# An image pipeline with medians and an attention: the pace of the inverse transform, the counts of the median, the engine of its masks

## The chip, the core and the metric

The kernel runs on one core of one Trainium2 chip. Its engines are TensorE (PE; weight loads are listed as PEld), VectorE (DVE), ScalarE (ACT), GpSimd (POOL) and SyncE (SP, which here only issues transfers). Each takes its instructions in a fixed order; what passes between them goes through semaphores. The metric is the device time of one launch in microseconds (us), with the median of several runs. The profile is of one execution more.

## What is computed

The input x is 16 images of 64 channels, 128 by 128, in float32. Layer 0 shifts each channel by its median where that is negative, doubles the resolution with a 7-tap filter, rectifies, and filters and halves it again. Layer 1 filters in the frequency domain and then runs an attention over all 16,384 pixels of an image with 320 keys.

```python
# layer 0
q_in = jnp.quantile(x.reshape(B, C, -1), 0.5, axis=-1)
x = x + jax.nn.relu(-q_in)[:, :, None, None]
y = upfirdn2d(x, lpf, up=2, padding=lpf.shape[0] - 1, gain=4.0)
y = jnp.maximum(y, 0.0)
x = upfirdn2d(y, lpf, down=2, padding=0, gain=1.0)
# layer 1
spec = jnp.fft.rfft2(x, norm='ortho')
mag = jnp.abs(spec)
hid = jax.nn.gelu(jnp.einsum('bchw,oc->bohw', mag, fg_w1), approximate=False)
gate = jax.nn.sigmoid(jnp.einsum('bchw,oc->bohw', hid, fg_w2))
xf = x + jnp.fft.irfft2(spec * gate, s=(h, w), norm='ortho')
...
out = (attention of the queries from xf over keys and values from strided convolutions of xf)
return out @ proj_w + proj_b + x
```

## The kernel before

There are two phases. `phase1` makes z (layer 0's output, stored in `zd`) and xf (stored in `xfd`); `phase2` is the attention. The change touches `phase1` alone.

**Units.** A group is four channels of one image (G = 4, so NG = 16 groups per image). Partitions hold image rows or, later, frequencies. The program's main loop runs over steps u; an image has U = 32 of them, two per group, and v = u % 32 is the step within the image.

**A group's way.** `load` (L351) brings the group's four channels into one of four "pad" buffers by a GpSimd transfer (L355), and GpSimd adds the shift (L357). `up_cols` (L362) filters along the columns into `up`: two ScalarE instructions (L372), five on VectorE (L374). `up_rows`, once per half group, multiplies by the filter matrix on PE (L384, L393) and rectifies on ScalarE into `r` (L386) and `rc` (L395). `down_rows` goes back with PE (L407, L410) and copies y on ScalarE (L413), once per half group. `down_cols` (L415) makes z in seven VectorE instructions (L424, L426) and stores it through SP's queue (L429). `fourier_rows` (L437, copied at L439) and `fourier_cols` (PE at L448 to L451, copied by ScalarE into `sp`, L453) make the spectrum; 22 of these `sp` buffers exist. In a step the program writes down `load` for the group two ahead and `up_cols` for the group one ahead.

**The gate.** `gate(b)` is a generator, begun in step v = 5 of the next image, one piece per step. For each group it squares and adds (L463 on ScalarE, L465 and L466 on GpSimd) and takes the root into `mag` (L467, ScalarE). Then come PE transposes and two small products, and a sigmoid into `gt` (L515, L523). `mag` and `gt` of all images share one buffer (tag "maggt").

**The inverse.** For a group, `open_gate` (L530) works on GpSimd: 1 + gate (L534), the product with both parts of the spectrum (L536, two instructions), two small ones (L538, L539). It is kept behind the newest shift (`issue_after`). `inverse_cols` is 8 products on PE (L549) and a copy `bt` (L557); `inverse_rows` 4 more (L568), a ScalarE copy into `xf` (L576, two buffers) and the store by GpSimd's queue (L579). In the loop a group goes through these three in successive steps, one group per step: the gates of groups 0 to 15 are opened in steps 14 to 29 of the image after.

**The medians.** `medians(b)` is a generator for two images (128 channels on 128 partitions). SP loads both halves of the pixels into `xm` (L169; one buffer each, 2 MB per transfer, four transfers). A first guess comes from 2,048 pixels. Then `count` (L183: four VectorE passes of 4,096 values, each with its sum) counts the values under a threshold: twice for the two ends, then FINE = 5 times, with a new threshold from a secant each time (L270 to L275, L280 to L282). The last threshold t lies within a few ranks of the median. For each of 16 slices of 1,024 values (NS = 8 per half) VectorE then masks what is not below t (L289, L290) and takes the eight largest (L292); all this uses one buffer (tag "hit"), which the counts use too. From these candidates come the two middle values (L297 to L306). A flag says if some row ended more than 7 ranks off or hid a candidate; it goes through memory (L317, L319, L321), is read by VectorE's sequencer, and where it is set a full bitwise `search` of 33 counts follows. Last the shift is written and spread over the partitions (L334, L336, `sb`). `medians(0)` runs alone before the loop; the others are written down piece by piece in the steps from every even image on, for the images two ahead.

**The order.** The program text gives priorities; the order of the instructions on each engine is laid out when the kernel is built, by a planner that goes by those priorities and by when it thinks that operands and buffers are ready. So a piece can stand well before its place in the text: in the trace a median's L272 stands between two passes of the count written before it, and the last median is done when about 9 of the 16 images are.

Of the kernel before, what the change touches and what calls it, by code (L numbers as in the profile page):

```python
# [8 lines left out]
F32 = mybir.dt.float32  # L9
# [3 lines left out]
ALU = mybir.AluOpType  # L13
# [4 lines left out]
B, C, H, W = 16, 64, 128, 128  # L18
# [12 lines left out]
PAD = 3  # L31
# [2 lines left out]


GOAL, MISS = RANK + 9, 7
FINE = 5
BIG = 3.0e38


# [89 lines left out]
def phase1(ctx, tc, nc, cs, ident, x, w1, dram, zd, xfd):  # L130

    G = 4
    NG = C // G
    wp = ctx.enter_context(tc.tile_pool(name="p1w", bufs=1))
    big = ctx.enter_context(tc.tile_pool(name="p1big", bufs=1))
# [3 lines left out]
    io = ctx.enter_context(tc.tile_pool(name="p1io", bufs=3))  # L139
# [21 lines left out]
    def medians(b):  # L161
# [3 lines left out]
        for f in range(2):  # L165
            t = big.tile([128, HALF], F32, name=f"xm{b}_{f}", tag=f"xm{f}")
# [33 lines left out]
            nc.vector.tensor_scalar(less, total, float(RANK), None, ALU.is_gt)  # L200
            return less

        NS = 8
        L = HALF // NS

        def search(low, high):
# [49 lines left out]
        for f in range(2):  # L256
            hit = big.tile([128, FEW], F32, name=f"more{b}_{f}", tag="hit")
# [26 lines left out]
        cand = small.tile([128, 16 * NS], F32, name=f"cand{b}", tag="cand")  # L284
        for f in range(2):
            for s in range(NS):
                up = big.tile([128, L], F32, name=f"down{b}_{f}{s}", tag="hit")
                cut = xm[f][:, s * L : (s + 1) * L]
                nc.vector.tensor_scalar(up, cut, t, -BIG, ALU.is_ge, ALU.mult)  # L289
                nc.vector.tensor_tensor(up, up, cut, ALU.add)  # L290
                j = 8 * (NS * f + s)
                nc.vector.max(cand[:, j : j + 8], up)  # L292
                if s % 2:
                    yield
        top = small.tile([128, 16], F32, name=f"top{b}", tag="top")
        rest = big.tile([128, 16 * NS], F32, name=f"rest{b}", tag="hit")
# [46 lines left out]

    shifted = []
    pads = []
    for i in range(4):
        t = wp.tile([128, G, W + 2 * PAD], F32, name=f"pad{i}", tag=f"pad{i}")
        nc.gpsimd.memset(t, 0.0)
        pads.append(t)

    def load(b, g):  # L351

        c0 = G * g
        xi = pads[g % 4][:, :, PAD : PAD + W]
        nc.gpsimd.dma_start(out=xi, in_=x[b, c0 : c0 + G].rearrange("c h w -> h c w"))  # L355
        shifted.append(
            nc.gpsimd.tensor_tensor(  # L357
                xi, xi, shifts[b][:, c0 : c0 + G].unsqueeze(2).to_broadcast([128, G, W]), ALU.add
            ).ins
        )  # L360

    def up_cols(b, g):  # L362

        src = pads[g % 4]
        up = work.tile([128, G, UP], F32, name=f"up{b}_{g}", tag="up")
        for odd in range(2):
            o = up.rearrange("p g (m t) -> p g m t", t=2)[:, :, :, odd]
            for j in range(4 - odd):
                s = src[:, :, PAD - j : PAD - j + UP // 2]
                w = taps[:, 2 * j + odd : 2 * j + odd + 1]  # L370
                if j == 0:
                    nc.scalar.activation(o, s, AF.Copy, scale=w)  # L372
                else:
                    nc.vector.scalar_tensor_tensor(o, s, w, o, ALU.mult, ALU.add)  # L374
        us[b, g] = up
# [39 lines left out]
    def down_cols(b, g):  # L415
        n = f"{b}_{g}"
        c0 = G * g
        y = ys.pop((b, g)).rearrange("p g (m t) -> p g m t", t=2)
        z = io.tile([128, G, W], F32, name=f"z{n}", tag="z")
        for k in range(7):  # L420
            s = y[:, :, k // 2 : k // 2 + W, k % 2]
            w = taps[:, 6 - k : 7 - k]
            if k == 0:
                nc.vector.tensor_scalar(z, s, w, None, ALU.mult)  # L424
            else:
                nc.vector.scalar_tensor_tensor(z, s, w, z, ALU.mult, ALU.add)  # L426
        zv = zd[b][c0 : c0 + G].rearrange("c h w -> h c w")
        for at, h, m in HOME:
            nc.sync.dma_start(out=zv[h : h + m], in_=z[at : at + m])  # L429
        zs[b, g] = z  # L430
# [129 lines left out]
    def inverse_rows(b, g):  # L560
        n = f"{b}_{g}"
        c0 = G * g
        bt = bts.pop((b, g))
        o_ps = banks(f"ops{n}")
        for r in range(2):
            for i in range(2):
                half = slice(64 * i, 64 * i + 64)
                nc.tensor.matmul(  # L568
                    o_ps[:, i, 0:256],
                    cs("ihs" if r else "ihc")[half],  # L570
                    bt[half, r].rearrange("p q w -> p (q w)"),
                    start=(r == 0),
                    stop=(r == 1),
                )
        xf = io.tile([128, G, W], F32, name=f"xf{n}", tag="xf", bufs=2)
        nc.scalar.copy(  # L576
            xf.rearrange("p (q i) w -> p i q w", i=2), o_ps[:, :, 0:256].rearrange("p i (q w) -> p i q w", q=2)
        )
        nc.gpsimd.dma_start(out=xfd[b][c0 : c0 + G].rearrange("c h w -> h c w"), in_=xf)  # L579
# [12 lines left out]
        load(0, g)  # L592
    up_cols(0, 0)
    running, net = None, None
    for u in range(B * U + FIRST + NG + 2):
        b, v = u // U, u % U
        if v == 0 and b % 2 == 0 and b + 2 < B:
            running = medians(b + 2)
# [9 lines left out]
        w = u - FIRST - U  # L608
        for k, stage in ((-1, open_gate), (0, inverse_cols), (1, inverse_rows)):
            q = w - k  # L610
            if q >= 0 and q % U < NG and q // U < B:

                with tc.issue_after(shifted[-1]) if k < 0 else nullcontext():
                    stage(q // U, q % U)
        if v % 2 == 0 and at(u + 2):
            up_cols(*at(u + 2)[:2])
        if at(u):
# [444 lines left out]
```

## Time and profile before

| what | us |
|---|---|
| median of three runs (11609.7 to 11617.6) | 11612.71 |
| the profiled execution, its own time | 11611.63 |
| its span | 11609.8 |
| VectorE busy, whole span | 8352.8 |
| PE busy, whole span | 10189.2 |
| GpSimd busy, whole span | 2502.4 |
| first y copied (ScalarE, L413) | 307.9 |
| last median's flag read (L321) | 3457.6 |
| last y copied | 5284.4 |

The profile is one execution, taken by the hardware profiler. Engine names are as above. A row gives line, engine, operation, output and input with partitions x elements, and a count; then busy time and the mean of one in ns, then the idle time of the engine just before these instructions and who ended it. The row of one tile has minimum, median and maximum of one in ns instead. Rows of waits have the total in us, how often, and the longest. A stage's row gives, for each engine, the busy us and the number of instructions, then the clock that was granted to PE as a share of the full one, and the share and rate of the DMA engines. A wait is put down to what came last by the records, which is now and then not the true cause.

### The profile page before, as it was taken

The numbers are of one execution on the slowest core, as the hardware profiler recorded it, in microseconds if no ns is written. First come the engines' busy times: TensorE is split into PE (matmuls) and PEld (weight loads), VectorE is DVE, ScalarE is ACT, GpSimd is POOL, SyncE is SP. The second block draws the span as 40 slices with busy tenths as digits, with TensorE's granted clock in tenths as the row PEclk, the third lists the DMA queues.
The fourth block names the chain that finished last, engine by engine and source line by source line (L and its number), as shares of the span: only waits on it lengthen the run. The fifth ranks groups of instructions, "written<-read, shape, count | busy, mean of one in ns | idle before, by whom it ended". The sixth has DMA issues, their size and how long they took to land.

```text
span 11609.8 us, 175376 instructions
## 1 busy us (share of the span) xinstructions
PE 10189.2 (88%) x68096; PEld 4603.2 (40%) x68096; DVE 8352.8 (72%) x12025; ACT 5524.1 (48%) x7585; POOL 2502.4 (22%) x3370
## 2 busy tenths in 40 slices
PE   0668777787889999996999999999999999999999
PEld 0445444444445555553333333333333333333333
DVE  6978879779795555551777767767777677676777
ACT  0435444444445555552444545545445455454555
POOL 0224333343334444442000000000000000000000
PEclk9889888888889999998999999999999999999999
DMA  2121221221211111113212121121121211210111
GB/s 54 38 61 48 57 67 40 66 62 41 64 40 48 48 47 48 45 45 86 61 34 61 38 58 38 39 58 37 33 63 39 58 37 38 58 39 30 37 39 31
DMA packets 462689, 560.44 MB, mean 48 GB/s; under 512 B 80904, under 2 KB 344464, under 8 KB 459536
## 3 DMA queue, kind: packets, MB, share of 16 engines
q1 hardware_dynamic: 396304, 347.68, 13.2%
q0 software_dynamic: 65536, 201.39, 5.6%
q8 instruction: 538, 8.81, 0.3%
q14 instruction: 311, 2.55, 0.1%
HBM read 343.36 MB, written 201.33 MB: 47 GB/s over the span
## 4 chain that ended last, share of the span: by engine, by line
PE 48%; ACT 5%; DMA 1%; DVE 1%; SPq 1%; issue 1%; POOL 1%; ACTq 0%; POOLq 0%; DVEq 0%
PE av L791 13%; PE ma L791 13%; PE ss L791 12%; ACT e L881 4%; PE qp L791 3%; PE pj L791 2%; PE cp L704 2%; SPq L682 1%; PE bps L549 0%; DMA q<-nt 0%; DMA xp<-xfd 0%; DVE sd L728 0%; POOL sp L536 0%; PE rps L384 0%; PE yps L407 0%
## 5 line engine op out<-in xcount | busy, mean ns | idle before, releaser
L791 DVE TENSOR_REDUCE nm<-ma 128x2 f32<-128x640 f32 x4096 | 3240.9, 812 | 1272.1 <-PE ss L791 804.2
L881 ACT ACTIVATE e<-ss 128x1024 f32<-128x1024 f32 x2560 | 2620.7, 1024 | 2840.1 <-PE ss L791 2812.7
L791 PE MATMUL ss<-q,kg 32*128 32x512 f32 (+1 forms) x12288 | 2843.4, 635 | 32.5 <-DMA q<-nt 32.3
L791 PE MATMUL ma<-kg,q 32*128 32x320 f32 x16384 | 2763.6, 475 | 21.3 <-DVE nm L791 19.5
L791 PEld LDWEIGHTS ma<-kg,q 32*128 32x128 f32 x16384 | 1187.4, 185 | 1543.8 <-ACT e L881 803.9
L791 PE MATMUL av<-e,vb 128*32 128x512 f32 (+1 forms) x10240 | 1673.5, 610 | 0.0
L384 PE MATMUL rps<-up,w1s 128*128 128x262 f32 x4096 | 1116.3, 412 | 632.5 <-DVE up L374 367.6
L426 DVE SCALAR_TENSOR_TENSOR z<-y,w1s,z 128x512 f32<-128x512 f32 x1536 | 1314.1, 856 | 31.6 <-DVEq L324 3.1
L374 DVE SCALAR_TENSOR_TENSOR up<-pad,w1s,up 128x524 f32<-128x524 f32 x1280 | 976.9, 809 | 410.1 <-ACT up L372 330.7
L791 PEld LDWEIGHTS ss<-q,kg 32*128 32x128 f32 (+1 forms) x12288 | 728.4, 166 | 1293.6 <-DVE nt L791 397.6
L384 PEld LDWEIGHTS rps<-up,w1s 128*128 128x128 f32 x4096 | 767.7, 199 | 890.2 <-DVE up L374 307.2
L407 PE MATMUL yps<-r,w1s 128*64 128x262 f32 x4096 | 629.5, 422 | 364.1 <-ACT xf L576 337.9
L932 POOL DMA_DIRECT2D result<-ot x512 | 267.4, 527 | 2785.6 <-DVE ot L791 2751.7
L807 POOL COPY xo<-xa 128x512 f32<-128x512 f32 x256 | 272.1, 1064 | 2529.3 <-issue 2319.8
L386 ACT ACTIVATE r<-rps 128x524 f32<-128x524 f32 x1024 | 609.9, 611 | 337.4 <-PE rps L384 337.1
L183 DVE TENSOR_SCALAR_CACHE_REDUCE hit<-xm,t 128x4096 uint8<-128x4096 f32 x160 | 715.8, 4474 | 2.5
L357 POOL TENSOR_TENSOR pad<-pad,sb 128x512 f32<-128x512 f32 x256 | 302.7, 1183 | 1362.6 <-DMA pad<-x 1064.1
L549 PE MATMUL bps<-csb,sp 128*64 128x256 f32 x4096 | 565.1, 424 | 33.0 <-POOL sp L538 33.0
L424 DVE TENSOR_SCALAR z<-y,w1s 128x512 f32<-128x512 f32 x256 | 138.6, 541 | 584.9 <-ACT y L413 580.9
L407 PEld LDWEIGHTS yps<-r,w1s 128*64 128x64 f32 x4096 | 268.4, 144 | 726.7 <-ACT xf L576 377.6
L467 ACT ACTIVATE mag<-q 128x260 f32<-128x260 f32 x256 | 167.8, 655 | 790.9 <-POOL q L466 527.0
L355 POOL DMA_DIRECT2D pad<-x x256 | 200.6, 784 | 1584.6 <-DVE up L374 444.9
(151 smaller groups left out, 11481.5 us busy)
## 6 DMA issues: line engine op xcount, KB each, us to landing
xm<-x SPq DMA_DIRECT2D x32, 2048.0 KB
pad<-x POOLq DMA_DIRECT2D x256, 256.0 KB, 5.3
xfd<-xf POOLq DMA_DIRECT2D x256, 256.0 KB, 5.1
xp<-xfd SPq DMA_DIRECT2D x128, 512.0 KB
xa<-xfd SPq DMA_DIRECT2D x512, 128.0 KB
zr<-zd SPq DMA_DIRECT2D x512, 128.0 KB
result<-ot POOLq DMA_DIRECT2D x512, 128.0 KB, 2.9
zd<-z SPq DMA_DIRECT2D x512, 122.0 KB
```

The lines of the kernel that those rows point to most:

```text
L183: nc.vector.tensor_scalar(hit, cut, thr, None, op, ALU.add, accum_out=cnt[:, j : j + 1])
L357: nc.gpsimd.tensor_tensor(xi, xi, shifts[b][:, c0 : c0 + G].unsqueeze(2).to_broadcast([128, G, W]), ALU.add).ins
L374: nc.vector.scalar_tensor_tensor(o, s, w, o, ALU.mult, ALU.add)
L384: nc.tensor.matmul(r_ps[:, i, 0:UP], ut[:, STAGES[k]], up[:, 2 * p + i, :], start=True, stop=True)
L386: nc.scalar.activation(t, r_ps[:, :, 0:UP], AF.Relu, scale=4.0)
L407: nc.tensor.matmul(y_ps[half, i, 0:UP], dr, r[k][:, i, :], start=True, stop=True)
L426: nc.vector.scalar_tensor_tensor(z, s, w, z, ALU.mult, ALU.add)
L549: nc.tensor.matmul(b_ps[64 * i : 64 * i + 64, 256 * q : 256 * q + 256], s[:, r, 2 * q + i, 0:64], cs("iv2" if r else "iv1"), start=(r == 0 ...
L791: last[engine] = op(*args, **kw).ins
L807: nc.gpsimd.tensor_copy(xo.rearrange("p (a e f) -> p a f e", e=8, f=16), xas[b, p].rearrange("p (a f e) -> p a f e", e=8, f=16),)
L881: nc.scalar.activation(e, s_ps, AF.Exp)
L932: nc.gpsimd.dma_start(out=ov[h][:, cut], in_=ot[64 * h : 64 * h + 64, :])
```

## The change

In the loop the inverse runs at two groups in every three steps: group 2k in step 3k and group 2k + 1 in step 3k + 1, so that 16 groups take 24 steps and the gates are opened in steps 14 to 36. The main loop gets eight steps more at its end for that. The medians count six times instead of seven (FINE = 4). The slices are half as long and twice as many (NS = 16, 32 slices of 512 values), their mask's two instructions go from VectorE to GpSimd and get a buffer of their own (tag "down", one), and a piece is now four slices instead of two, still eight pieces. There are three pads in place of four, taken in turn over the images' borders; z has two buffers in place of three, xf three in place of two.

```diff
--- before.py
+++ after.py
@@ -34,7 +34,7 @@
 
 
 GOAL, MISS = RANK + 9, 7
-FINE = 5
+FINE = 4
 BIG = 3.0e38
 
 
@@ -200,7 +200,7 @@
             nc.vector.tensor_scalar(less, total, float(RANK), None, ALU.is_gt)
             return less
 
-        NS = 8
+        NS = 16
         L = HALF // NS
 
         def search(low, high):
@@ -284,13 +284,13 @@
         cand = small.tile([128, 16 * NS], F32, name=f"cand{b}", tag="cand")
         for f in range(2):
             for s in range(NS):
-                up = big.tile([128, L], F32, name=f"down{b}_{f}{s}", tag="hit")
+                up = big.tile([128, L], F32, name=f"down{b}_{f}{s}", tag="down")
                 cut = xm[f][:, s * L : (s + 1) * L]
-                nc.vector.tensor_scalar(up, cut, t, -BIG, ALU.is_ge, ALU.mult)
-                nc.vector.tensor_tensor(up, up, cut, ALU.add)
+                nc.gpsimd.tensor_scalar(up, cut, t, -BIG, ALU.is_ge, ALU.mult)
+                nc.gpsimd.tensor_tensor(up, up, cut, ALU.add)
                 j = 8 * (NS * f + s)
                 nc.vector.max(cand[:, j : j + 8], up)
-                if s % 2:
+                if s % 4 == 3:
                     yield
         top = small.tile([128, 16], F32, name=f"top{b}", tag="top")
         rest = big.tile([128, 16 * NS], F32, name=f"rest{b}", tag="hit")
@@ -343,7 +343,7 @@
 
     shifted = []
     pads = []
-    for i in range(4):
+    for i in range(3):
         t = wp.tile([128, G, W + 2 * PAD], F32, name=f"pad{i}", tag=f"pad{i}")
         nc.gpsimd.memset(t, 0.0)
         pads.append(t)
@@ -351,7 +351,7 @@
     def load(b, g):
 
         c0 = G * g
-        xi = pads[g % 4][:, :, PAD : PAD + W]
+        xi = pads[(NG * b + g) % 3][:, :, PAD : PAD + W]
         nc.gpsimd.dma_start(out=xi, in_=x[b, c0 : c0 + G].rearrange("c h w -> h c w"))
         shifted.append(
             nc.gpsimd.tensor_tensor(
@@ -361,7 +361,7 @@
 
     def up_cols(b, g):
 
-        src = pads[g % 4]
+        src = pads[(NG * b + g) % 3]
         up = work.tile([128, G, UP], F32, name=f"up{b}_{g}", tag="up")
         for odd in range(2):
             o = up.rearrange("p g (m t) -> p g m t", t=2)[:, :, :, odd]
@@ -416,7 +416,7 @@
         n = f"{b}_{g}"
         c0 = G * g
         y = ys.pop((b, g)).rearrange("p g (m t) -> p g m t", t=2)
-        z = io.tile([128, G, W], F32, name=f"z{n}", tag="z")
+        z = io.tile([128, G, W], F32, name=f"z{n}", tag="z", bufs=2)
         for k in range(7):
             s = y[:, :, k // 2 : k // 2 + W, k % 2]
             w = taps[:, 6 - k : 7 - k]
@@ -572,7 +572,7 @@
                     start=(r == 0),
                     stop=(r == 1),
                 )
-        xf = io.tile([128, G, W], F32, name=f"xf{n}", tag="xf", bufs=2)
+        xf = io.tile([128, G, W], F32, name=f"xf{n}", tag="xf")
         nc.scalar.copy(
             xf.rearrange("p (q i) w -> p i q w", i=2), o_ps[:, :, 0:256].rearrange("p i (q w) -> p i q w", q=2)
         )
@@ -592,7 +592,7 @@
         load(0, g)
     up_cols(0, 0)
     running, net = None, None
-    for u in range(B * U + FIRST + NG + 2):
+    for u in range(B * U + FIRST + 3 * NG // 2 + 2):
         b, v = u // U, u % U
         if v == 0 and b % 2 == 0 and b + 2 < B:
             running = medians(b + 2)
@@ -608,10 +608,10 @@
         w = u - FIRST - U
         for k, stage in ((-1, open_gate), (0, inverse_cols), (1, inverse_rows)):
             q = w - k
-            if q >= 0 and q % U < NG and q // U < B:
+            if q >= 0 and q % U < 3 * NG // 2 and q % U % 3 < 2 and q // U < B:
 
                 with tc.issue_after(shifted[-1]) if k < 0 else nullcontext():
-                    stage(q // U, q % U)
+                    stage(q // U, 2 * (q % U // 3) + q % U % 3)
         if v % 2 == 0 and at(u + 2):
             up_cols(*at(u + 2)[:2])
         if at(u):
```

## The prediction

> **What bounds the kernel now.** I read the page first (its 40 slices), then the busy time by stage, then in each stage the waits by engine, then single rows. One table gives the stages:
>
> ```profile
> core 0: us, PE busy (x) PEld busy (x) DVE busy (x) ACT busy (x) POOL busy (x), PEclk, DMA share, GB/s
> 0.00:290.00 290.00, 0.00 (x0) 0.00 (x0) 195.02 (x197) 1.28 (x1) 5.32 (x12) 1.00 0.26 54
> 290.00:3450.00 3160.00, 2431.61 (x13725) 1474.89 (x13725) 2649.86 (x3178) 1440.96 (x2533) 1068.98 (x1373) 0.87 0.22 54
> 3450.00:5290.00 1840.00, 1689.18 (x10160) 1022.78 (x10158) 1012.30 (x1272) 1040.75 (x1827) 824.47 (x1084) 0.96 0.16 46
> 5290.00:5500.00 210.00, 106.69 (x661) 57.41 (x663) 15.40 (x30) 45.54 (x66) 60.73 (x110) 0.73 0.44 103
> 5500.00:11609.00 6109.00, 5961.74 (x43558) 2048.15 (x43552) 4480.25 (x7350) 2995.52 (x3160) 542.89 (x792) 0.98 0.18 44
> ```
>
> The reader is to see five stages. Up to 290 the first median runs alone. From 290 to 3450 the seven other medians run beside the images: 300 copies of y by ScalarE fall there, so a half group takes 3160/300 = 10.53 us. From 3450 to 5290 no median is left: 212 half groups, 8.68 us each, PE busy 1689 of 1840 (92%). Then the inverse of the last image, and the attention, which the change leaves alone. At the later pace 300 half groups would take 2604 us, so the medians cost at most 556 us of the second stage; that is the prize. Inside it, four stretches of counting (770 us in all) show VectorE busy 761 and PE 568, and five stretches of masks (530 us) VectorE 509, PE 438, GpSimd 227. VectorE is the bound while it counts; under the masks PE is near its own limit too. Between two medians nearly everything stands, for transfers and behind them:
>
> ```profile
> DVE sums L253 <- DMA xm<-x: 187.1, 11, 25.7
> ...
> ACT xf L576 <- DMA xfd<-xf: 105.0, 19, 14.5
> ...
> PE yps L407 <- ACT xf L576: 278.8, 48, 29.2
> ...
> ACT mag L467 <- POOL q L466: 365.7, 99, 19.6
> ```
>
> These are waits of the second stage (total us, times, longest). ScalarE has waited 105 us for a buffer of xf to be stored, and PE 279 us for y's partner behind such a copy.
>
> **The change, part by part.** All sums stand against the profiled execution: 11611.63 us with a span of 11609.8; the median of the runs, 11612.71, is 1.1 above it. The prices of the median are in these rows (the first three of the second stage, the others over phase 1):
>
> ```profile
> L290 DVE TENSOR_TENSOR down<-down,xm 128x1024 f32<-128x1024 f32 x112 | 144.1, 1287 | 0.7
> L292 DVE MAX8 cand<-down 128x8 f32<-128x1024 f32 x112 | 136.4, 1218 | 0.7
> ...
> L289 DVE TENSOR_SCALAR down<-xm,t 128x1024 f32<-128x1024 f32 x112 | 92.8, 828 | 0.7
> ```
>
> ```profile
> L357 POOL TENSOR_TENSOR pad<-pad,sb x256: 1028/1035/3173, 290.9 to 5174.0; 128x512 f32<-128x512 f32 x128
> ```
>
> ```profile
> L534 POOL TENSOR_SCALAR gt<-gt 128x260 f32<-128x260 f32 x256 | 255.4, 1005 | 29.0 <-ACT gt L523 29.0
> L465 POOL TENSOR_TENSOR q<-sp 128x260 f32<-128x260 f32 x256 | 195.7, 769 | 138.8 <-ACT sp L453 136.9
> ```
>
> (1) The first median. One count is four passes of 4.48 us plus the small steps to the next threshold; in the timeline the rounds begin at 95.04 and 115.53, so one count less gives 20.5 us. Masks and maxima ran from 195.14 to 248.11, 53.0 us for 16 slices of 1,024. Now there are 32 slices of 512, and with one buffer named "down" each goes strictly round: mask on GpSimd (two instructions), maximum on VectorE, then the next mask. The tensor-tensor at 512 is between 1.03 us (L357, quietest) and 1.42 (L536's 0.72 at 260 elements, scaled). No GpSimd row has a tensor-scalar with two operations and a pointer. Quiet L534 takes 0.85 us at 260; to 512 elements that is 1.26 by the slope of the two-input rows (1.03 less 0.62, the quiet L465, for 252 elements) or 1.67 in proportion; if the second operation doubles it, 3.3. The maximum at 512 is 0.68, on the line between 1.22 at 1,024 and 0.28 at 128. Two hand-overs make 0.1 (a GpSimd result reached ScalarE in 0.04). A slice is thus 3.1 to 3.9 us, 5.5 if doubled; 32 of them 98 to 124 us, 177 if doubled. Net: +25 to +50, at worst +104. I take +37: single-operation rows are the nearest. Nothing covers this: no image can begin before its shift.
>
> The GpSimd rule speaks against the move. The Trainium skill ("GPSIMD Engine Reference", 4.1 Engine selection) sends elementwise work to VectorE, with GpSimd about twice as slow for two inputs; its section 3.1 gives 4497 ns for 2,048 elements, so 1.12 us for 512 by proportion, an estimate. By that price alone the 32 additions of a median would cost 3 us more than by L357's row.
>
> (2) Counts in the second stage: seven medians, 20 us of VectorE each, from stretches where VectorE is 99% busy and PE 74%. A stretch of about 192 us becomes 172 with PE at 83%, still under the 92% of the later stage, so the time comes back whole: −140. Bounds: 0 if transfers set the medians' pace anyway, −140.
>
> (3) Masks in the second stage: VectorE loses (144.1+136.4+92.8)/7 = 53.3 us per median and keeps 32 × 0.68 = 21.8. But in those stretches (106 us each) PE is busy 87.6; at 92% it needs 95. At most 11 us per median come back: −77. Bounds 0 and, were VectorE alone the bound, 7 × 31.5 = −220.
>
> (4) What the masks bring to GpSimd: 32 × (2.3 to 3.1) = 73 to 99 us per median, beside the 45 us that it already does in such a stretch. Over the stage GpSimd goes from 1069 of 3160 to about 1700: not a bound by total. But GpSimd and VectorE now pass one buffer to and fro 32 times, both in fixed order. Behind a waiting maximum stand z and up on VectorE, for which PE waits; behind a waiting mask stand the pad load's issue and shift, the gate's opening and xf's store. The nearest row for an engine that waits for a GpSimd pair is ScalarE's mag: 365.7 us for the 150 of this stage, 2.4 us each. ScalarE is 46% busy and often has nothing else; VectorE is full, and its order has z and up to put in between. I take a quarter, 0.6 us for each of 224 maxima: +134. Bounds 0 and 2.4 × 224 = +546.
>
> The two engines also slow each other. L536 has a median of 720 ns and a maximum of 1719, L374 739 at least and 1553 at most, and the timeline has such pairs side by side near 1090. The same page (8. Key points) names it: a shared SBUF interface, contended by VectorE instructions with two SBUF inputs. No sum here uses the rule; the rows are in the +134.
>
> (5) A third buffer for xf: ScalarE's waits for its store, 105.0 us, and 47.7 in the later stage, would mostly go. Behind them PE lost up to 278.8 and 59.1, though some of that has other causes and part comes back as the next wait, for pad or xm. I take −65 (about 35 of the later stage's 59, 30 before). Bounds 0 and −153.
>
> (6) The pacing. No instruction is added or removed. The later stage has 151 us of idle PE, 92 without the waits of (5), much of it in steps that had no inverse in them; the 16 inverse groups now fill 24 of 32 steps. Against it: the gate array and the magnitudes share one buffer, and its last reader moves from step 29 to 36, one step ahead of the next gate. More than the present 8 of the 16 magnitudes then come in a burst (1.08 us of ScalarE, about 1.4 of GpSimd each) in which PE loses about 8 us. I take −20; bounds −92 and +100 (6 us for each of 16 images).
>
> (7) Three pads and two z. In the later stage a pad load starts as soon as its pad's last reader ends (3851.05, then 3851.62), so up to three groups ahead, and takes some 7 us with its shift; at two groups ahead 17 us of a slack of about 45 are lost. With two buffers z is written again 29 us after it was finished (3845.4, 3874.1); its Fourier rows are done by 3866.3, and its store, whose landing no row shows, is half the size of xf's, which lands in 5.1. The cover is gone where xm jams the DMA (one pad load took 47.5 us): +5, bounds 0 and +50.
>
> Sum: 37 − 140 − 77 + 134 − 65 − 20 + 5 = −126. 11611.6 − 126 = **11,485 us**.
>
> **The rivals.**
> *VectorE stands at the maxima* (the slow side). If each of the 224 maxima waits 1.8 us (three quarters of mag's row), (4) is 403 and not 134: 11,485 + 269 = **11,755**. It decides from 260/224 = 1.16 us per maximum on (260 being all gains less all other losses). For it: the 1159–1185 stretch, where ScalarE waited 24.55 us for an opened gate that was itself queued on GpSimd behind a pad's 17.81 us wait; more GpSimd work lengthens such queues. Against: fillers.
> *VectorE was the bound throughout*: then all 7 × 51.5 = 361 us come back, xf's 153 too, with half of (4): 11,611.6 + 37 − 361 − 153 + 67 − 20 + 5 = **11,187**. For it: VectorE at 96% even under the masks. Against: PE at 83% there.
> *Hidden anyway*: transfers (187 us for xm, 105 for the flags' way through memory) set how fast medians follow; (2), (3) and (5) give nothing, (4) nothing either. Left are 37 − 20 + 5: **11,634**.
> *It does not do what it says*: with six counts a row could end over 7 ranks off, and the full search would run, 33 counts of 20 us, some 650 us. I followed the counts in float32 on the reference's input: the furthest of the 1,024 rows ends 6 off, so no search. 1 in 100.
>
> **How the numbers follow.** Forecast 0.50, standing maxima 0.27, VectorE throughout 0.13, hidden 0.09, search 0.01. The time is the forecast's, 11,485. The range leaves out about 1 in 10 on each side: 11,210 (just past the fast rival's time) to 11,780 (just past the slow one). The forecast's own range, its mid values varied singly, is 11,350 to 11,620. 0.2% is 23 us, about what can be told from no change. Faster: 0.44 of the forecast's 0.50 and all 0.13, so 0.57; no change: 0.03 of the forecast, 0.04 of hidden and 0.01 of the standing maxima, 0.08; slower: the rest, 0.35.
>
> **What would show it.** Right: the first pad shift starts at 320 to 345 instead of 290.9; L183 has 192 passes instead of 224; the mask rows on POOL have means of 2.3 to 3.1 us together; the last median's flag comes well before 3457; waits for xfd in front of xf fall under 50 us; VectorE's waits in front of its maximum stay under 200 us. Wrong: over 260 us there; a mask pair over 4 us; mag's waits for sp over the present 263; a later stage slower than 8.68 us per half group, which would put the fault with the pacing and the shared buffer; or any search.

## The result, and the profile after

The changed kernel takes 11939.66 us (median of four runs, 11936.31 to 11947.19) against 11614.1 for the kernel before beside it: ratio 1.0281, 95% interval [1.0264, 1.0299], 326 us slower. The forecast was 11,485, with a range up to 11,780: direction and range were both missed. The profiled span is 11934.5. The stages of the trace, in the columns used before (the second ends with the last median's flag, which fell at 3600.3 instead of 3457.6; it is cut 17 us before the first shift, which adds 0.06 us to each y below):

```profile
core 0: us, PE busy (x) PEld busy (x) DVE busy (x) ACT busy (x) POOL busy (x), PEclk, DMA share, GB/s
0.00:318.00 318.00, 0.00 (x0) 0.00 (x0) 146.40 (x160) 1.28 (x1) 108.31 (x74) 1.00 0.18 38
318.00:3600.00 3282.00, 2260.48 (x12212) 1382.67 (x12212) 2217.01 (x2722) 1302.80 (x2260) 1679.85 (x1654) 0.82 0.20 48
3600.00:5612.00 2012.00, 1910.95 (x11583) 1163.86 (x11583) 1220.59 (x1469) 1200.78 (x2091) 1003.69 (x1247) 0.97 0.16 49
```

The second stage makes 269 copies of y in 3282 us, 12.20 each where it was 10.53. VectorE, which was to be relieved and so let PE go faster, is busy 68% of it instead of 84%, PE 69% instead of 77%, GpSimd 51% instead of 34%. Over the whole stage nobody is the bound by busy time; everybody waits. The later stage has become better: 243 copies in 2012 us, 8.28 each where it was 8.68. So the loss is in the stage with medians, but for some 45 us in front of the first shift. The stretches in which the masks are used show more than the stage. These are sums over the seven later medians, each from its first maximum to its last, before and then after:

```profile
sum 769.04, PE 644.91 PEld 391.08 DVE 729.32 ACT 396.93 POOL 304.92; mean PE 92.13 PEld 55.87 DVE 104.19 ACT 56.70 POOL 43.56
```

```profile
sum 1237.34, PE 775.78 PEld 474.16 DVE 632.00 ACT 433.99 POOL 1071.97; mean PE 110.83 PEld 67.74 DVE 90.29 ACT 62.00 POOL 153.14
```

84 copies of y fall into the first and 89 into the second: 468 us more for about the same work on the images. VectorE was the full engine there (95%, GpSimd 40%); now GpSimd is (87%, VectorE 51%). The stage's waits, VectorE's, then PE's, then ScalarE's (total us, times, longest):

```profile
DVE cand L292 <- POOL down L290: 601.3, 195, 14.5
DVE sums L253 <- DMA xm<-x: 194.7, 11, 27.7
DVE z L424 <- DMA zd<-z: 74.3, 11, 13.3
```

```profile
PE fps L437 <- DVE z L426: 553.1, 70, 30.5
...
PE yps L407 <- ACT xf L576: 79.0, 18, 11.5
```

```profile
ACT y L413 <- DVE z L426: 463.5, 63, 30.3
...
ACT mag L467 <- POOL sp L536: 185.6, 7, 37.4
```

The two rows behind z were, in the stage before:

```profile
PE fps L437 <- DVE z L426: 142.9, 28, 12.6
```

```profile
ACT y L413 <- DVE z L426: 117.4, 24, 13.0
```

VectorE stands 601 us in front of its maxima, 2.7 us for each of the 224 of this stage. PE's wait for z has grown from 142.9 to 553.1, ScalarE's from 117.4 to 463.5: z stands behind the maximum on VectorE. Two things went as wanted: PE's wait behind xf fell from 278.8 to 79.0, and in this stage no wait of xf for its store is left. The tile of the masks (ns: minimum, median, maximum), and who held it up:

```profile
L289 POOL TENSOR_SCALAR down<-xm,t x256: 1991/2346/3104, 155.8 to 3578.1; 128x512 f32<-128x512 f32 x128
L290 POOL TENSOR_TENSOR down<-down,xm x256: 1252/1265/1721, 157.9 to 3581.2; 128x512 f32<-128x512 f32 x128
L292 DVE MAX8 cand<-down x256: 671/695/697, 160.1 to 3583.4; 128x8 f32<-128x512 f32 x128
its engine sat idle before it (us, times) until:
  POOL down L290: 697.5, 223
  DVE t L275: 151.9, 3
  DVE cand L292: 140.7, 142
```

Two stretches of the timeline show the round trip (start, us, engine and line, and in brackets the idle time before it with its releaser). In the first median, with nothing else on the chip:

```profile
204.25 0.69 DVE L292 MAX8 cand<-down 128x8 f32<-128x512 f32 x1 [3.47 <-POOL down L290]
205.04 2.00 POOL L289 TENSOR_SCALAR down<-xm,t 128x512 f32<-128x512 f32 x1 [0.83 <-DVE cand L292]
207.12 1.26 POOL L290 TENSOR_TENSOR down<-down,xm 128x512 f32<-128x512 f32 x1
208.41 0.69 DVE L292 MAX8 cand<-down 128x8 f32<-128x512 f32 x1 [3.47 <-POOL down L290]
```

and beside the images, VectorE alone:

```profile
3509.12 1.06 DVE L426 SCALAR_TENSOR_TENSOR z<-y,w1s,z 128x512 f32<-128x512 f32 x1
3512.34 0.69 DVE L292 MAX8 cand<-down 128x8 f32<-128x512 f32 x1 [2.16 <-POOL down L290]
3512.95 1.83 DVE L426 SCALAR_TENSOR_TENSOR z<-y,w1s,z 128x512 f32<-128x512 f32 x2
3516.93 0.69 DVE L292 MAX8 cand<-down 128x8 f32<-128x512 f32 x1 [2.15 <-POOL down L290]
3517.54 0.73 DVE L426 SCALAR_TENSOR_TENSOR z<-y,w1s,z 128x512 f32<-128x512 f32 x1
3521.52 0.69 DVE L292 MAX8 cand<-down 128x8 f32<-128x512 f32 x1 [3.25 <-POOL down L290]
```

A quiet slice takes 4.17 us (204.25 to 208.41): 2.00 + 1.26 on GpSimd, 0.69 on VectorE, and small gaps. Later VectorE has fillers (z), but only one or two between two maxima, and z's seven instructions are spread over several slices. One z began at 3532.60 and had five of its seven instructions behind it at 3544.38; by the medians of its instructions (486 ns for L424, 752 for L426) its seven take 5.0 us. PE's L437 waits for its end.

### The profile page after: what moved, and what is told of

The parts are those of the page before. It is cut to its first block, busy times and chain, and to the rows that moved or that the text cites. A ratio compares the mean times of both kernels' runs of the same rounds, so it can differ in the third digit from the quotient of the medians.

```text
span 11934.5 us, 176032 instructions
## 1 busy us (share of the span) xinstructions
PE 10252.5 (86%) x68096; PEld 4660.6 (39%) x68096; DVE 8080.5 (68%) x11729; ACT 5551.7 (47%) x7585; POOL 3398.2 (28%) x3881
## 4 chain that ended last, share of the span: by engine, by line
PE 59%; ACT 6%; POOL 3%; DVE 2%; issue 2%; DMA 1%; SPq 1%; ACTq 0%; DVEq 0%; POOLq 0%
PE av L791 13%; PE ma L791 13%; PE ss L791 12%; ACT e L881 4%; PE rps L384 3%; PE qp L791 3%; PE pj L791 2%; PE cp L704 2%; PE yps L407 2%; PE bps L549 2%; PE yps L410 1%; PE fps L437 1%; PE ops L568 1%; PE cps L393 1%; DMA pad<-x 1%
## 5 line engine op out<-in xcount | busy, mean ns | idle before, releaser
L384 PE MATMUL rps<-up,w1s 128*128 128x262 f32 x4096 | 1134.6, 419 | 527.4 <-DVE up L374 466.0
L426 DVE SCALAR_TENSOR_TENSOR z<-y,w1s,z 128x512 f32<-128x512 f32 x1536 | 1377.2, 897 | 43.8 <-DVEq L324 8.0
L374 DVE SCALAR_TENSOR_TENSOR up<-pad,w1s,up 128x524 f32<-128x524 f32 x1280 | 997.8, 833 | 248.1 <-ACT up L372 244.2
L384 PEld LDWEIGHTS rps<-up,w1s 128*128 128x128 f32 x4096 | 779.9, 202 | 823.6 <-DVE up L374 389.4
L437 PE MATMUL fps<-csb,z 128*128 128x128 f32 x2048 | 375.4, 339 | 586.9 <-DVE z L426 553.1
L289 POOL TENSOR_SCALAR down<-xm,t 128x512 f32<-128x512 f32 x256 | 593.8, 2320 | 300.7 <-DVE t L275 151.9
L413 ACT COPY y<-yps 128x524 f32<-128x524 f32 x512 | 305.6, 597 | 753.2 <-DVE z L426 463.5
L292 DVE MAX8 cand<-down 128x8 f32<-128x512 f32 x256 | 177.5, 693 | 697.5 <-POOL down L290 697.5
L424 DVE TENSOR_SCALAR z<-y,w1s 128x512 f32<-128x512 f32 x256 | 136.3, 532 | 694.5 <-ACT y L413 596.0
L437 PEld LDWEIGHTS fps<-csb,z 128*128 128x128 f32 x2048 | 318.1, 237 | 685.3 <-DVE z L426 430.8
```

What stands on the lines that cost most here:

```text
L289: nc.gpsimd.tensor_scalar(up, cut, t, -BIG, ALU.is_ge, ALU.mult)
L384: nc.tensor.matmul(r_ps[:, i, 0:UP], ut[:, STAGES[k]], up[:, 2 * p + i, :], start=True, stop=True)
L413: nc.scalar.copy(ys[b, g][:, 2 * p : 2 * p + 2, :], y_ps[:, :, 0:UP])
L437: nc.tensor.matmul(f_ps[:, 128 * i : 128 * i + 128], z[:, i, :], cs("fh"), start=True, stop=True)
```

## The experiments

Times are given against the kernel before in the same series of runs (11,601 to 11,616), with the ratio's 95% interval. They fall into four questions.

### Which part of the change loses the time?

`masks_on_vector` is the kernel after with L289 and L290 on VectorE again, all else as in the change:

```diff
-                nc.gpsimd.tensor_scalar(up, cut, t, -BIG, ALU.is_ge, ALU.mult)
-                nc.gpsimd.tensor_tensor(up, up, cut, ALU.add)
+                nc.vector.tensor_scalar(up, cut, t, -BIG, ALU.is_ge, ALU.mult)
+                nc.vector.tensor_tensor(up, up, cut, ALU.add)
```

> The changed kernel with the two mask instructions back on VectorE, all else kept (six counts, pacing, 32 slices, buffers). Theory HANDOVER: the loss is made where VectorE stands at each maximum for GpSimd's mask, 697.5 us over the eight medians; without that wait the kernel falls below the kernel before: its own gain in the stage after the medians, 0.4 us for each of 512 half groups (205), plus about 20 us for each of eight counts less (160), so 11,614 - 365 = 11,250, range 11,180 to 11,350. Rival PACING-OR-BUFFERS: the stage with medians is slow because of the later inverse, three pads or two z buffers (VectorE waited 74 us for the store of z there); then it stays above 11,614, near 11,800.

Measured: 11417.26, 0.9839 [0.9823, 0.9856], 191 us faster than before and 516 better than the change against it. The masks' engine is the whole loss and more. HANDOVER's range (11,180 to 11,350) was still missed: the rest of the change gains less than it took.

The other parts were put into the kernel before one by one. `masks_alone` has NS = 16, the masks on GpSimd in their own buffer, and three pads; `pacing_alone` only the two groups in three steps; `six_counts_alone` only FINE = 4; `xf_buffers_alone` two buffers for z and three for xf; `three_parts` is all but the masks (counts, pacing, z and xf; four pads and NS = 8 kept).

> The kernel before with only the mask's move to GpSimd, 32 slices and their own buffer (and three pads, which make the room for it): seven counts, no pacing, three z, two xf. Theory BOTH: the first median grows by 65 (45 measured plus the count that is kept), the hand-over and the queue cost as in the changed kernel, 520: 11,614 + 520 = 12,135, range 12,030 to 12,260. Rival TOGETHER (the masks only hurt with the paced inverse, whose opened gates stand between them): under 11,900.

> The kernel before with only the inverse at two groups in three steps. Theory HANDOVER has the pacing (with xf's third buffer) as the gain: 8.68 to 8.28 us per half group in the stage without medians; by pacing alone two thirds of 205 us, so 11,480, range 11,400 to 11,560. Rival PACING-OR-BUFFERS: the later inverse makes the magnitudes come in a burst and costs 6 us per image: 11,610 to 11,750.

> The kernel before with six counts in place of seven and nothing else. By the prediction's step 2: 20.5 us in front of the loop and 20 us for each of seven medians, 11,606 - 160 = 11,446, range 11,430 to 11,500. Rival: three_parts lay only 50 us under pacing_alone with the counts and xf's buffer on top, so most of the counts' time is hidden behind xm and the flags: 11,560, range 11,530 to 11,590.

> The kernel before with two z and three xf buffers. By the prediction's step 5, xf's third buffer gives 65: 11,540. Rival: the third buffer is paid for by z's second, as VectorE then waits about 100 us for z's store (95.6 and 102.0 in two runs): 11,590 to 11,640.

> The kernel before with six counts, the pacing, two z and three xf buffers; four pads, 16 slices and masks on VectorE as before. HANDOVER: the best of the versions, 11,614 - 365 and a little less for the fourth pad, 11,200, range 11,130 to 11,320. PACING-OR-BUFFERS: above 11,614.

| kernel | us | ratio | against before, us |
|---|---|---|---|
| masks_alone | 12105.36 | 1.0431 [1.0414, 1.0449] | +501 |
| pacing_alone | 11507.86 | 0.9918 [0.9901, 0.9934] | −100 |
| six_counts_alone | 11526.56 | 0.9936 [0.992, 0.9953] | −75 |
| xf_buffers_alone | 11598.80 | 0.9997 [0.9987, 1.0006] | −3 |
| three_parts | 11457.35 | 0.9873 [0.9857, 0.989] | −151 |

The four parts alone add up to +323, and the whole change measured +326. The three gains together fall 27 short of their own sum (−151 for −178), so they overlap somewhat, but one part carries the sign. masks_alone and pacing_alone came out inside their ranges; three_parts stayed well above its own (11,130 to 11,320); the counts and xf's buffers came out as their rivals said (the counts 3 us under the rival's 11,530). masks_on_vector is 40 us faster than three_parts, from which it differs by three pads, shorter slices and the masks' own buffer; which of these gains was not tested.

### Is it the hand-over, or GpSimd's work?

Three kernels keep the change and cut the masks down. In `no_handover` GpSimd computes every mask, but the maximum reads the raw slice, so that nobody waits for a mask. In `no_masks` the two instructions are gone too. In `light_masks` the tensor-scalar is left out and the other stays, so that each mask costs 1.26 us instead of some 3.6 and all 256 hand-overs remain. (In all three the candidates are not the masked ones, and the test for a hidden candidate is left out.)

```diff
-                nc.vector.max(cand[:, j : j + 8], up)
+                nc.vector.max(cand[:, j : j + 8], cut)
```

> The changed kernel where the maxima read the unmasked pixels, so that nobody waits for the masks that GpSimd still makes, and the test for a hidden candidate is left out: the medians come out wrong, the work on every engine is otherwise that of the changed kernel. Theory HANDOVER: the wait is the loss, so the time falls like that of the kernel with masks on VectorE or lower, 11,150 to 11,350. Rival LOAD: it is GpSimd's 600 + 320 us of mask work that delays shifts, opened gates and stores, or slows VectorE at the shared memory port; then it stays above 11,614, near 11,850.

> The changed kernel without any mask: the maxima read the pixels themselves and the test for a hidden candidate is left out, so the medians come out wrong. It differs from the run without hand-over only by GpSimd's mask work, and from the one with masks on VectorE by 32 x 1.18 us of VectorE per median. Theory BOTH (hand-over 188 us, mask work queued on GpSimd about 330): 11,417 less what is left of 302 us of VectorE, so 11,330, range 11,230 to 11,420; the mask work then costs 11,752 - 11,330 = 420. Rival HANDOVER ALONE (the 334 us between 11,752 and 11,417 come from another order of the instructions, not from GpSimd's work): it stays near 11,700.

> The changed kernel with the tensor-scalar of each mask left out and the addition kept (it adds the slice to itself; medians wrong, the hidden test left out): the hand-overs stay 32 per median, GpSimd's work per slice falls from 3.6 to 1.27 us. Theory BOTH: work and wait both fall to about a third, so a third of the 520 us between 11,940 and 11,417 is left: 11,590, range 11,480 to 11,680. Rival COUNT OF HAND-OVERS (each costs by its crossing, whatever the mask takes): 11,750 and more.

Measured: no_handover 11751.67, 1.0127 [1.011, 1.0144], +144 against before; no_masks 11266.11, 0.971 [0.9694, 0.9726], −339; light_masks 11441.38, 0.9854 [0.9837, 0.987], −163. From the change's +326 the hand-over thus makes 182, and GpSimd's work, when no maximum waits for it any more, still 482; 148 of that is given back against masks_on_vector, since VectorE has no masks to do (326 − 182 − 482 + 148 is −190, where masks_on_vector stands). light_masks looks from another side: with every hand-over kept and a third of the work, the masks cost 175 instead of 664. The two prices do not simply add: 182 and a third of 482 would be 343. They hold for this order of taking things away, and without the wait the masks also stand closer together than in the change. LOAD's condition for no_handover (above 11,614) held, no_masks fell into the range of BOTH, and light_masks came out below its range (11,480 to 11,680). The wait that heads the list of VectorE's waits was 601 us, yet removing it gave 182. Why, is seen in GpSimd's own timeline in no_handover:

```profile
1820.10 2.00 POOL L289 TENSOR_SCALAR down<-xm,t 128x512 f32<-128x512 f32 x1
1823.46 1.04 POOL L356 TENSOR_TENSOR pad<-pad,sb 128x512 f32<-128x512 f32 x1 [1.36 <-DMA pad<-x]
1824.59 0.87 POOL L533 TENSOR_SCALAR gt<-gt 128x260 f32<-128x260 f32 x1
1825.42 1.26 POOL L290 TENSOR_TENSOR down<-down,xm 128x512 f32<-128x512 f32 x1
1826.64 1.42 POOL L535 TENSOR_TENSOR sp<-sp,gt 128x260 f32<-128x260 f32 x2
1828.16 2.01 POOL L289 TENSOR_SCALAR down<-xm,t 128x512 f32<-128x512 f32 x1
1830.13 0.21 POOL L537 TENSOR_TENSOR sp<-sp 128x4 f32<-128x4 f32 x1
...
1835.25 2.00 POOL L289 TENSOR_SCALAR down<-xm,t 128x512 f32<-128x512 f32 x1
1837.33 1.26 POOL L290 TENSOR_TENSOR down<-down,xm 128x512 f32<-128x512 f32 x1
1838.53 0.82 POOL L578 DMA_DIRECT2D xfd<-xf  x1
1839.35 0.75 POOL L354 DMA_DIRECT2D pad<-x  x1
```

GpSimd has hardly a gap: in 1702 to 1840 it is busy 131 of 138 us (PE 58). So it is in all seven later medians, from the first mask's start to the last one's end:

```profile
sum 971.79, PE 442.71 PEld 266.75 DVE 530.76 ACT 210.29 POOL 921.07; mean PE 63.24 PEld 38.11 DVE 75.82 ACT 30.04 POOL 131.58
```

GpSimd is 95% busy, PE 46%, and 48 copies of y fall into 972 us, 20 us for each half group. The gate's opening (L533 to L537), the pad's shift (L356), the pad's load (L354) and xf's store (L578) each stand among masks, in the one order of this engine. The next shift begins only at 1862.40, after 21.55 us of waiting for its load. That load was issued at 1839.35, just behind the next two loads of xm (1838.62); from 1840 to 1862 the DMA engines are 95% busy, so this last wait is in part the transfer's. ScalarE's longest wait for an opened gate is 78.9 us in this kernel, 37.4 in the change. So the wait for the mask was replaced by waits for what is queued among the masks. The medians do end sooner without it (last flag at 2932.6 instead of 3600.3), but until then a half group takes 12.3 us, as in the change (12.1); in no_masks it takes 10.5.

### Which of GpSimd's other work is late?

With and without masks, the opening of the gates was moved to VectorE (the four lines L534 to L539, and no order behind the shift), then the squares too (L465, L466). The pairs leave out of the medians what no_masks and no_handover do.

```diff
-            nc.gpsimd.tensor_tensor(q2, specs[b, g][:, 1], specs[b, g][:, 1], ALU.mult)
-            nc.gpsimd.tensor_tensor(q1, q1, q2, ALU.add)
+            nc.vector.tensor_tensor(q2, specs[b, g][:, 1], specs[b, g][:, 1], ALU.mult)
+            nc.vector.tensor_tensor(q1, q1, q2, ALU.add)
...
-        nc.gpsimd.tensor_scalar(gg, gg, 1.0, None, ALU.add)
+        nc.vector.tensor_scalar(gg, gg, 1.0, None, ALU.add)
```

> The run without masks, with the gate's opening (five instructions per group) on VectorE instead of GpSimd and not kept behind the newest shift. It is the reference of the next run: about 345 us more of VectorE, of which half is in the later stage where it has room; 11,266 + 0 to 150.

> The run without hand-over, with the gate's opening on VectorE as in the run beside it, so that only shifts, squares and transfers are queued among GpSimd's masks. Theory GATE: the masks cost 486 us (11,752 less 11,266) because the opened gates stand among them, and ScalarE, whose next magnitudes wait for the last opened gate, holds up PE (longest wait 78.9 us); then the difference to the run without masks falls to 0 to 200. Rival SHIFT-AND-PORT: pad loads, shifts and the shared memory port make the cost; then 350 or more of the 486 stay.

> The kernel after without the medians' masks (the maxima read the raw slice, and the test for a hidden candidate is left out, so the medians of rows that need a mask are others), with the opening of the gates and, new here, the squares of the gate (L465, L466) on VectorE. Base for the next run. Against gate_vector_no_masks (11,255) VectorE gets 512 more instructions of 260 elements, some 0.3 to 0.4 us each by its 512-element additions of 0.7, so 150 to 200 us of work, of which the share in stages with PE at its limit is hidden: 11,230 to 11,330 by either theory.

> The same with the masks computed on GpSimd but the maxima reading the raw slice (nobody waits for a mask; the test for a hidden candidate is left out). Nothing of the gate is left in GpSimd's queue: beside the masks only the shifts with their pad loads and the issue of xf's stores. Theory QUEUE (what is left of the masks' price after the gate opening went to VectorE, 11,548 - 11,255 = 294 us, is squares and roots standing behind masks): the difference to squares_vector_no_masks falls under 120 us. Rival SHIFT (pad loads, shifts and xf stores behind the masks cost as much, or the masks slow the other engines' memory access): it stays above 200. Between 120 and 200: both.

| on GpSimd beside the masks | without masks, us | with masks, nobody waiting, us | price of the masks |
|---|---|---|---|
| opening, squares, shifts, transfers | 11266.11 (0.971 [0.9694, 0.9726]) | 11751.67 (1.0127 [1.011, 1.0144]) | 482 |
| squares, shifts, transfers | 11254.88 (0.9699 [0.9683, 0.9715]) | 11548.36 (0.9955 [0.9938, 0.9972]) | 293 |
| shifts, transfers | 11081.05 (0.9539 [0.9523, 0.9555]) | 11323.60 (0.9749 [0.9732, 0.9765]) | 243 |

The prices are differences of what each stands against its own kernel before. Opened gates made 189 of the 482 (293 lies between GATE's 200 and the 350 of SHIFT-AND-PORT, so neither had it alone), the squares 50. In both kernels of the second and third row the opening is also no longer held behind the shift; that was not tried by itself. The two kernels without masks came out faster than the spans given for them, gate_vector_no_masks only 8 us faster than no_masks, which is not clear of the noise. For the last pair QUEUE expected under 120 and SHIFT over 200: SHIFT held. ScalarE's waits in the second stage of squares_vector_no_handover have a row that the same kernel without masks hasn't:

```profile
ACT up L371 <- POOL pad L356: 139.0, 11, 30.2
```

The shift that the next group needs stands behind masks; the longest of these waits is 30 us, 12.8 of which the shift itself waits for its pad's load. 42 us more lie in the first median, whose first shift also stands behind 30 of the 32 masks (266.6 against 224.3). If both count in full, which the 601 us above didn't, about 60 of the 243 are left without a row. They may be slower access: z's two-input instructions (mean of one, last number before the idle time) in squares_vector_no_handover, then without masks:

```profile
L425 DVE SCALAR_TENSOR_TENSOR z<-y,w1s,z 128x512 f32<-128x512 f32 x1536 | 1293.7, 842 | 19.1 <-DVEq L323 2.8
```

```profile
L422 DVE SCALAR_TENSOR_TENSOR z<-y,w1s,z 128x512 f32<-128x512 f32 x1536 | 1231.0, 801 | 18.8 <-DVEq L320 2.6
```

That is 63 us of VectorE over the whole phase; what of it reaches the end was not separated.

`two_down_buffers` is the change with two buffers for the mask, paid for with xf's third one:

```diff
-                up = big.tile([128, L], F32, name=f"down{b}_{f}{s}", tag="down")
+                up = big.tile([128, L], F32, name=f"down{b}_{f}{s}", tag="down", bufs=2)
...
-        xf = io.tile([128, G, W], F32, name=f"xf{n}", tag="xf")
+        xf = io.tile([128, G, W], F32, name=f"xf{n}", tag="xf", bufs=2)
```

> The kernel after with two buffers for the mask (down) and, to make room, two for xf instead of three, nothing else. ROUND TRIP (the one buffer, by which each mask must wait for the maximum before it, makes the 188 us that no_handover gained): most of it comes back, 11,760 to 11,820 (xf's third buffer was worth 3 us by itself together with the z's). MASK TIME (the maximum waits for 3.3 us of GpSimd's own work, which a second buffer does not shorten): 11,880 to 11,960, and VectorE's waits in front of its maxima stay over 400 us.

Measured: 11857.02, 1.0207 [1.019, 1.0224], +241: 85 us better than the change with xf's third buffer given up, between the two theories' spans, so neither is right alone. VectorE still waits 438.1 us in front of its maxima in this stage (601.3 in the change), over the 400 that MASK TIME named: most of the wait is not for the buffer.

### What beats both kernels?

`vector_masks_z3` is the change with its masks on VectorE (in the counts' buffer, tag "hit") and three buffers for z. `best_squares_vector` has the squares on VectorE too, `best_gate_vector` the opening of the gates as well, not held behind the shift. All three compute everything.

> The changed kernel with the masks on VectorE and in the old buffer; the 2 KB that this frees go to a third z. The run with masks on VectorE showed 95.6 us of VectorE's waits for z's store; if these are on the path, 11,417 falls to 11,330 (range 11,290 to 11,390); if they only stand for the next wait (xm, flags), it stays within 20 us of 11,417.

> The kernel of vector_masks_z3 (the change with its masks on VectorE and three buffers for z; 11,409) with the squares of the gate (L465, L466) on VectorE too; everything is computed. Theory QUEUE SERVES MAG (ScalarE's mag stands behind squares on a slow GpSimd, and PE behind ScalarE): without masks squares and opening together gave 11,266 - 11,081 = 185 us, opening alone 11; so most of it comes here: 11,220 to 11,300. Rival FULL VECTOR (VectorE has no room, counts and masks being on it): 11,360 to 11,480.

> The same with the opening of the gates on VectorE as well (and not kept behind the newest shift); everything is computed. By QUEUE SERVES MAG 11,200 to 11,290; by FULL VECTOR slower than best_squares_vector by 20 to 100, since 256 times five more instructions stand on VectorE.

Measured: 11408.70, 0.9834 [0.9817, 0.985]; 11313.28, 0.9751 [0.9735, 0.9767]; and 11142.85, 0.9604 [0.9588, 0.962]. Each step in the direction opposite to the change gained: 92 us for the squares and 170 more for the opening, though FULL VECTOR had it that VectorE has no room (the first step ended 13 us above QUEUE SERVES MAG's range, the second 57 below it). Giving z its third buffer changed little (within 20 us of masks_on_vector), so z's waits for its store were not on the path. The last kernel from 318 to 3400, which lies within its stage with medians (the last flag falls at 3688.8):

```profile
core 0: us, PE busy (x) PEld busy (x) DVE busy (x) ACT busy (x) POOL busy (x), PEclk, DMA share, GB/s
318.00:3400.00 3082.00, 2579.58 (x14910) 1564.71 (x14908) 2713.99 (x4375) 1570.67 (x2743) 427.88 (x468) 0.90 0.23 57
```

VectorE is busy 88% and PE 84%, at a granted clock of 0.90; GpSimd, left with shifts and issues, is busy 14%. This kernel is 458 us faster than the one before and 784 faster than the change, each taken against its own kernel before.

## Why the prediction was wrong, step by step

The step that failed is **(4)**, "I take a quarter, 0.6 us for each of 224 maxima: +134". The mechanism was in the text, as the slow side's rival, with its point of decision at 1.16 us per maximum; measured were 601.3/224 = 2.7 us, above even the 2.4 of the nearest row. It can also be put by the runs: masks_alone cost 501, of which 63 lie before the first shift (353.8 against 290.9). With step (3)'s −77 and (7)'s +5, (4) had to be 501 − 63 + 77 − 5 = 510, near its upper bound of 546. What failed in it:
- "its order has z and up to put in between". The timeline shows one or two of them per slice of over 4 us, and they are just what the fillers delay, since PE waits for the whole z.
- "not a bound by total" was judged over the stage, where the share came as forecast (about 1700 of 3160; measured 1679.85 of 3282, 51%). But the same paragraph gives 73 to 99 us of masks beside 45 us of other work, 118 to 144 us of GpSimd in a stretch of 106 us: by its own numbers GpSimd was the bound under the masks. Measured, the seven stretches grew from 769 to 1237 us, with GpSimd busy 87%.
- Step (4) priced only the hand-over. It named what stands behind a waiting mask, and gave it nothing. The runs show that 482 us hang on GpSimd's work even when no maximum waits for a mask.

The slow rival's time, 11,755, had the mechanism right and a price of 1.8 us; at 2.7 it would have been 11,485 − 134 + 601 = 11,952. That this lies so near to 11,940 is partly chance, since only 182 of the change's loss went with the wait itself. The other two rivals' times, 11,187 and 11,634, both lie far below the measured one.

The other steps:
- **(1)** the number right, in part by luck. The first shift came at 335.5, +44.6 where +37 was taken and 25 to 50 given. Within it the quiet tensor-scalar took 2.00 us, above the 1.26 to 1.67 taken from single-operation rows (the tensor-tensor, 1.26, lay inside its 1.03 to 1.42), so a slice 4.17 and not 3.1 to 3.9; 32 of these are 133 us, and the net would have been about +60. What saved the sum was not in it: the masks began at 155.8, beside the last count, which no mask needs.
- **(2)** too large, and not come back in the way foreseen: −140 was taken besides 20.5 in the first median. six_counts_alone gave 75 in all, 23 of it before the first shift, so 52. Its last flag came 251 us earlier (3206.9), but until then a half group took 10.50 us, as before (10.49): the medians ended sooner, the images beside them went no faster, and only 22 half groups more fell into the quicker stage. About a third of the prize was there, and "so the time comes back whole" was wrong. ScalarE's waits for xf's store grew from 152.8 to 192.8 up to the last y; what part that has was not tested.
- **(3)** near. With the masks gone altogether (no_masks against masks_on_vector) 148 us came back, 56 of them before the first shift (223.1 against 279.0). That leaves 92 as the most that this relief is worth; 77 was taken.
- **(5)** too large: −3 with z's two buffers instead of −65 and +5. xf's waits for its store fell as predicted (152.8 to 53.6), but PE's wait behind xf only from 278.8 to 235.2, so the store wasn't its main cause; and z began to wait for its own store, 54.1 us where no such row was. "Its store, whose landing no row shows" was the weak place of (7).
- **(6)** too small: −20 taken, −100 measured, a little past the bound of −92. In pacing_alone the 210 half groups behind the last flag take 8.23 us each, where the same number took 8.70 before: 98 us. Until the flag the pace is as before (10.44, 10.49). The burst of magnitudes that was set against it doesn't show. Why it is worth so much was not tested.
- **(7)** not tested alone: three pads came only with the shorter slices and the masks' own buffer. masks_on_vector, which has all of these, is the faster beside three_parts, so no loss shows.

Of the signs that were named: 192 passes of L183, the first shift, the waits of xf, the later stage and the absence of a search came as forecast; ScalarE's mag waited 242 us for sp, under the 263; the mask pair's mean, 2.32 + 1.31 = 3.63 us, passed the forecast's 3.1 and stayed under its 4; VectorE's 601 us in front of the maxima (wrong from 260 on) and the late last flag told that (4) had failed. One reading in (4) is off without effect: 720 ns is the minimum of L536, its median is 732.

## What to carry to other kernels

When work is moved to an idle engine, look at that engine's share in the stretch where the work will lie, not over the stage, and list all that it does there for others: each of those things will stand in the queue behind the new work, and that may cost more than the hand-over itself. A wait's total is no price: removing 601 us of waiting gave 182, because the other things in the same queue were still late. A nearly full engine that does work in the order needed can be a better place than one at a third that answers late: here the masks, the squares and the opening of the gates, moved to VectorE in this order, each gained.

## What the runs showed of the hardware

- GpSimd's tensor-scalar with two operations and a pointer took 2.00 us at 128x512 in float32 in the quiet, more than its tensor-tensor (1.26, and 1.03 for the shift, L357, of the same size). What VectorE does beside it matters: beside the count's passes, which read one tensor, the tensor-scalar still took 2.01 (median of 12); beside the instructions of z and up (L426, L374), which read two, 2.41 (median of 158), at most 3.10. The tensor-tensor L290 went from 1.26 to 1.64 in the same way (medians of 206 and 37).
- A hand-over between the two engines is cheap by itself: in the quiet rows about 0.03 us from GpSimd's end to VectorE's start and 0.1 back (204.25 + 0.69 to 205.04).
- The granted PE clock was lower where PE waited more: 0.82 in the change's second stage (PE busy 69%), 0.87 before (77%), 0.90 in best_gate_vector from 318 to 3400 (84%). The same matmul (L384, 128x262) took 437, 419 and 411 ns on average there, so part of a loss by waiting shows as slower matmuls. That the waits lower the clock, and not the reverse, fits these runs but was not tested.
